# A graph kernel's pre-activations taken from PSUM by one ScalarE copy, with VectorE's sums a piece later in SBUF, and f1 left in a PSUM bank

## The chip, the cores and the metric

The kernel runs on one core of a Trainium2 chip. The metric is the device time of one execution, in microseconds. An engine is named as the profile names it: PE is TensorE, DVE is VectorE, ACT is ScalarE, POOL is GpSimd, SP is SyncE (here it only issues DMAs); PEld is PE's weight load. SBUF is the on-chip memory, PSUM the banks into which PE writes its products, 128 partitions by 512 float32 numbers each.

## What is computed

The input x has 32 entries of 512 nodes by 256 features; adj is one sparse 512 by 512 adjacency matrix with weights. Four layers follow one another; layers 0 and 3 are the same function with different weights, and they are the ones the change is about:

```python
def gnn(h, A, W1, b1, W2, b2, Wa, ba, Wm, bm, beta1, beta2, beta3):   # layers 0 and 3
    pre_u = einsum('bud,dk->buk', h, W1[:d])
    pre_v = einsum('bvd,dk->bvk', h, W1[d:])
    hidden = relu(pre_u[:, :, None, :] + pre_v[:, None, :, :] + b1)
    S = sigmoid(einsum('buvk,ko->buvo', hidden, W2)[..., 0] + b2[0])
    a = einsum('buv,bud->bvd', S * A, h)
    m = einsum('uv,bud->bvd', A, h) * h
    return beta1 * h + beta2 * (a @ Wa + ba) + beta3 * (m @ Wm + bm)

x = gnn(x, adj, ...)                                   # layer 0
x = x + relu((adj @ x) @ W.T + b)                      # layer 1
feats = x @ W1.T; f1 = feats @ W2 + b2                 # layer 2
coefs = softmax(leaky_relu(f1[:, :, None] + f1[:, None, :]) + adj)
x = coefs @ feats + bias2 + x
x = gnn(x, adj, ...)                                   # layer 3
```

S is needed only where adj is not zero: at the edges. The kernel computes it there alone.

## The kernel before

The 32 entries are worked on in eight groups of four (`NB = 4`). A group goes through five streams of work:

- `first` (layer 0, one entry after the other): x is loaded (h0), turned by PE (`turned`, L536) and copied to hT by ACT (L537), stored for later (the DMA xT<-hT, L730), and then `pre` computes pre_u and pre_v.
- `edges` of layer 0: POOL fetches rows of pre_v, one row for each edge and all four entries at once, by an indirect DMA (`fetch`, L582, rows<-table); the partner rows of pre_u come as "mine" by SP (L622) or POOL. DVE adds the two (L654, 128x1024) and takes relu, times W2, summed over features (L667, four times 128x256). After a few items ACT takes exp (L567) and DVE the sigmoid (L571, L572) and the product with the edge's weight (L611), and POOL puts the result into a dense table of cells by an indirect DMA (`put`, L576).
- `middle`: SP loads the dense cells (`load`, L689, SA<-cells), and for each entry `middle_one` does the rest of layer 0, layers 1 and 2, and at its end `pre` for layer 3, from the entry's xT.
- `edges` of layer 3, the same as before with other weights.
- `last`: the rest of layer 3, and the store to the output.

`pre` (L540) is where the change lies. For each of the four chunks of 128 nodes, which the texts call a piece, PE writes pre_u and pre_v side by side into one PSUM tile (pst, 128x512). Then, in order: DVE writes pre_u + b1 into an SBUF tile puv (L549, reading PSUM); ACT copies pre_v into its other half (L550, reading PSUM); DVE adds pre_v, from PSUM, and pre_u + b1 (L552); DVE takes relu, times W2, summed (L553), for the diagonal of S. The DMA that writes puv to the table in HBM (L557, issued by SP) is kept in `self.later` and given out by `settle` at the next piece. There are 8 groups x 2 layers x 4 entries x 4 chunks = 256 pieces. puv has three buffers, shared by `first` and `middle`; `both` has one.

In `middle_one`, f1 (layer 2, one number for each node, spread over the partitions) is written by PE into a PSUM tile and copied to SBUF by ACT (L835); four ACT instructions for each entry read it (L851), each followed by DVE's leaky_relu (L852).

How the order comes about: the streams are Python generators. `sparse_path` gives each of their pieces a share of work, and each stream a start and an end in units of a group's period; `weave` sorts all pieces by the time that follows. Streams marked "fill" (`first`, `last`) are not given out at their time but held, up to eight pieces, and put in where `middle` says that PE would stand still. So `first` of the next group and `last` of the former one run beside `middle` and `edges`. A framework then takes the instructions, orders them for each engine by what it expects of their times, and puts in the semaphores; each engine and each DMA queue works through its own list in order. An instruction that has to wait therefore holds all that stands behind it on its engine. The texts use "boundary" for the place in each period where `first` of the next group ends and the edges of layer 0 begin.

Of the kernel before, what the change touches and what calls it, by code (L numbers as in the profile page):

```python
# [8 lines left out]
F32 = mybir.dt.float32  # L9
# [3 lines left out]
ALU = mybir.AluOpType  # L13
AX = mybir.AxisListType
PSUM = bass.MemoryType.PSUM

P = 128
N = 512
D = 256
NC = N // P  # L20
DC = D // P
# [18 lines left out]
def mm(nc, out, pairs):  # L40

    for n, (lhsT, rhs) in enumerate(pairs):
        nc.tensor.matmul(out, lhsT, rhs, start=(n == 0), stop=(n == len(pairs) - 1))  # L43


class Model:


    def __init__(self, ctx, tc, a):
        nc = self.nc = tc.nc  # L50
        self.tc, self.a = tc, a
        const = self.const = ctx.enter_context(tc.tile_pool(name="const", bufs=1))
        self.ident = const.tile([P, P], F32, name="ident")
        make_identity(nc, self.ident)
        self.adj = const.tile([P, NC, N], F32, name="adj")
        for c in range(NC):
            nc.sync.dma_start(self.adj[:, c, :], a["adj"][c * P : (c + 1) * P, :])
        self.g0, self.g3 = self.gnn_first("L0_gnn"), self.gnn_first("L3_gnn")
# [352 lines left out]
def by_two(t, n=2):  # L411
    return t.rearrange("p (c d) -> p c d", c=n)


class Sparse:
# [3 lines left out]
    def __init__(self, ctx, m, counts, xr, outr, B):  # L419
        self.m, self.nc, self.tc, self.counts = m, m.nc, m.tc, counts  # L420
        tc = m.tc
        self.xr, self.outr = xr, outr
        pool = lambda n, b, **k: ctx.enter_context(tc.tile_pool(name=n, bufs=b, **k))
        self.dram = pool("dram", 1, space=bass.MemoryType.DRAM)

        self.cells = {
            k: [self.dram.tile([CELLS + SPARE, NB], F32, name=f"cells_{k}{q}") for q in range(2)] for k in "03"
        }
        self.lists = self.dram.tile([N, 2 * N], F32, name="lists")
        self.x2s = self.dram.tile([B, P, NC, D], F32, name="x2s")  # L430

        self.xT, self.x2T = (self.dram.tile([B, P, DC, N], F32, name=n) for n in ("xT", "x2T"))
        self.e = Edges(m, pool("edges", 1))
        self.adjT = pool("adjT1", 1).tile([P, NC, N], F32, name="adjT")
        self.grp = pool("grp", 2)
        self.act, self.small, self.gath = pool("act", 1), pool("small", 2), pool("gath", 5)
        self.ps = pool("ps", 8, space=PSUM)
        self.later, self.bigs, self.given = None, 0, None

    def psum(self):  # L440
        return self.ps.tile([P, N], F32, name="pst", tag="pst")
# [97 lines left out]

    def pre(self, g, b, hT):  # L540

        nc, w = self.nc, g.w
        rows = g.table.rearrange("(c p k) (b d) -> p c k b d", p=P, k=2, b=NB)
        for c in range(NC):
            cs = slice(c * P, (c + 1) * P)
            pp = self.psum()
            mm(nc, pp, [(hT[:, d, cs], w["W1"][:, d::DC, :]) for d in range(DC)])
            puv = self.small.tile([P, 2, D], F32, name="puv", bufs=3)
            nc.vector.tensor_tensor(puv[:, 0, :], pp[:, 0:D], w["b1bc"], ALU.add)  # L549
            nc.scalar.copy(puv[:, 1, :], pp[:, D:])  # L550
            both = self.small.tile([P, D], F32, name="both", bufs=1)
            nc.vector.tensor_tensor(both, pp[:, D:], puv[:, 0, :], ALU.add)  # L552
            nc.vector.scalar_tensor_tensor(  # L553
                both, both, 0.0, w["W2bc"], ALU.max, ALU.mult, accum_out=g.self_s[:, c, b : b + 1]
            )
            self.settle()
            self.later = lambda c=c, puv=puv: nc.sync.dma_start(rows[:, c, :, b, :], puv)  # L557
            yield

    def settle(self):  # L560
# [226 lines left out]
    def middle_one(self, g0, g3, b, i, SA, keep, given):  # L787
        nc, m, w = self.nc, self.m, g0.w
        act, small, psum = self.act, self.small, self.psum
# [34 lines left out]
        yT = act.tile([P, DC, N], F32, name="yT")  # L824
# [4 lines left out]
            nc.vector.tensor_tensor(yT[:, c, :], yT[:, c, :], zT[:, c, :], ALU.add)  # L829
            yield c == DC - 1  # L830

        f1 = small.tile([P, N], F32, name="f1", bufs=1)
        pf = psum()
        mm(nc, pf, [(m.q_bc[:, c, :], yT[:, c, :]) for c in range(DC)])
        nc.scalar.copy(f1, pf)  # L835
        feats = act.tile([P, NC, D], F32, name="feats", tag="mhT0")
        eT = act.tile([P, NC, N], F32, name="eT")
        if more:
# [443 lines left out]
```

## Time and profile before

| | |
|---|---|
| median of 3 runs | 3247.94 us (3246.24 to 3251.05) |
| the profiled execution, its own time | 3230.9 us |
| its span in the profile | 3229.2 us |
| granted TensorE clock, mean | 0.928 |
| table<-puv, 256 issues of 256 KB: issue to landing | 2.4 us least, 4.9 median, 15.1 most |

The profile is of one execution. Its page gives the busy time of each engine, the chain of work that ended last, and groups of instructions: line, engine, operation, output tile <- input tile, shapes, count, then the busy time in us and the mean of one in ns, then the idle time of the engine just before them and what ended it. "<-DVE puv L549 376.2" in a row of ACT means: ACT stood idle for 376.2 us in all before these instructions, until a DVE instruction of L549 was done. SPq is SP's queue, the place where DMA issues wait.

### The profile page before, as it was taken

The numbers are of one execution on the slowest core, as the hardware profiler recorded it, in microseconds if no ns is written. First come the engines' busy times: TensorE is split into PE (matmuls) and PEld (weight loads), VectorE is DVE, ScalarE is ACT, GpSimd is POOL, SyncE is SP. The second block draws the span as 40 slices with busy tenths as digits, with TensorE's granted clock in tenths as the row PEclk, the third lists the DMA queues.
The fourth block names the chain that finished last, engine by engine and source line by source line (L and its number), as shares of the span: only waits on it lengthen the run. The fifth ranks groups of instructions, "written<-read, shape, count | busy, mean of one in ns | idle before, by whom it ended". The sixth has DMA issues, their size and how long they took to land.

```text
span 3229.2 us, 32451 instructions
## 1 busy us (share of the span) xinstructions
PE 2773.2 (86%) x8646; PEld 1656.2 (51%) x8646; DVE 2371.6 (73%) x7692; ACT 1007.0 (31%) x2341; POOL 1488.3 (46%) x1248
## 2 busy tenths in 40 slices
PE   6346887989997999979999899979998899999947
PEld 3223444546554566435654565536654465545626
DVE  7777736989596976969598786969688695953662
ACT  4452333322233222333223232333223222232441
POOL 1565402747264543636354462636355362630371
PEclk9677898999999999989999999989999999999969
DMA  8876425777567766776577766776577765640663
GB/s 273 295 246 229 152 91 166 261 262 224 188 226 240 234 196 202 249 241 220 173 230 235 245 203 211 237 250 207 178 219 246 242 221 190 219 159 33 209 201 112
DMA packets 302718, 679.40 MB, mean 210 GB/s; under 512 B 52672, under 2 KB 170944, under 8 KB 294336
## 3 DMA queue, kind: packets, MB, share of 16 engines
q0 software_dynamic: 111168, 338.90, 32.8%
q1 hardware_dynamic: 186224, 334.68, 31.0%
q10 hardware_dynamic: 5136, 3.68, 0.4%
q8 instruction: 71, 1.16, 0.1%
q14 instruction: 119, 0.97, 0.1%
HBM read 531.12 MB, written 146.01 MB: 210 GB/s over the span
## 4 chain that ended last, share of the span: by engine, by line
PE 38%; DVE 34%; DMA 17%; issue 6%; ACT 3%; POOL 1%; SPq 0%; ACTq 0%; POOLq 0%; DVEq 0%
PE pst L43 28%; DVE rows L667 11%; DVE rows L654 10%; DMA rows<-table,iv 6%; DMA table<-puv 4%; PE pst L945 4%; PE pst L802 2%; DMA cells<-s,cell 2%; PE pst L954 1%; DVE ex L852 1%; PE pst L896 1%; DMA cells<-self_s 1%; PE pst L809 1%; DVE ex L854 1%; DMA mine<-table,iu 1%
## 5 line engine op out<-in xcount | busy, mean ns | idle before, releaser
L582 POOL DMA_INDIRECT rows<-table,iv x554 | 680.1, 1228 | 1047.4 <-DMA table<-puv 383.1
L576 POOL DMA_INDIRECT cells<-s,cell x576 | 684.3, 1188 | 592.7 <-DMA cells<-s,cell 357.0
L654 DVE TENSOR_TENSOR rows<-rows,mine 128x1024 f32<-128x1024 f32 x554 | 667.3, 1215 | 195.0 <-DMA rows<-table,iv 178.9
L667 DVE SCALAR_TENSOR_TENSOR rows<-rows,L_gnn_W2bc 128x256 f32<-128x256 f32 x2016 | 750.9, 413 | 0.4
L43 PE MATMUL pst<-adj,h 128*128 128x512 f32 x1024 | 453.5, 592 | 0.0
L43 PE MATMUL pst<-L_gnn_Wa,hT 128*128 128x256 f32 x1024 | 260.6, 408 | 142.4 <-DMA hT<-xT 69.4
L43 PE MATMUL pst<-w_L_gnn_W,hT 128*128 128x512 f32 x512 | 261.2, 646 | 57.4 <-ACT hT L537 46.3
L43 PEld LDWEIGHTS pst<-adj,h 128*128 128x128 f32 x1024 | 192.8, 190 | 219.5 <-issue 214.1
L43 PEld LDWEIGHTS pst<-L_gnn_Wa,hT 128*128 128x128 f32 x1024 | 207.8, 208 | 187.8 <-issue 103.2
L43 PE MATMUL pst<-w_L_gnn_W,yT 128*128 128x512 f32 x512 | 239.9, 622 | 66.0 <-DVE yT L874 66.0
L43 PE MATMUL pst<-eT,feats 128*128 128x512 f32 x512 | 240.0, 624 | 9.1 <-ACT eT L897 9.1
L43 PE MATMUL pst<-adjT,zW 128*128 128x512 f32 x512 | 225.9, 592 | 0.0
L550 ACT COPY puv<-pst 128x256 f32<-128x256 f32 x256 | 94.7, 372 | 412.5 <-DVE puv L549 376.2
L945 PEld LDWEIGHTS pst<-hWa,SA 128*128 128x128 f32 x896 | 213.4, 328 | 5.9 <-issue 3.3
L945 PE MATMUL pst<-hWa,SA 128*128 128x256 f32 x896 | 216.2, 397 | 0.0
L43 PEld LDWEIGHTS pst<-w_L_gnn_W,yT 128*128 128x128 f32 x512 | 101.8, 200 | 196.3 <-issue 111.0
L549 DVE TENSOR_TENSOR puv<-pst,bc_L_gnn_b 128x256 f32<-128x256 f32 x256 | 106.6, 417 | 127.4 <-PE pst L43 64.4
L771 ACT COPY flat<-SA 128x512 f32<-128x512 f32 x128 | 134.5, 1122 | 203.3 <-PE pst L43 178.8
L802 PE MATMUL pst<-flat,hWa 128*128 128x512 f32 x448 | 196.8, 592 | 0.0
L43 PEld LDWEIGHTS pst<-w_L_gnn_W,hT 128*128 128x128 f32 x512 | 102.0, 206 | 168.0 <-issue 90.5
L43 PE MATMUL pst<-WT,hT 128*128 128x256 f32 x512 | 141.8, 434 | 38.8 <-DVE hT L810 38.8
L896 PE MATMUL pst<-ident,ex 128*128 128x128 f32 x512 | 88.5, 302 | 99.2 <-DVE ex L857 62.6
(167 smaller groups left out, 3728.0 us busy)
## 6 DMA issues: line engine op xcount, KB each, us to landing
table<-puv SPq DMA_DIRECT2D x256, 256.0 KB, 4.9
SA<-cells SPq DMA_DIRECT2D x64, 1024.0 KB, 7.0
h<-in_x_dram SPq DMA_DIRECT2D x64, 512.0 KB, 6.6
mine<-table SPq DMA_DIRECT2D x64, 512.0 KB, 6.2
hT<-xT SPq DMA_DIRECT2D x36, 512.0 KB, 5.0
h<-x2s SPq DMA_DIRECT2D x36, 512.0 KB, 6.1
xT<-hT SPq DMA_DIRECT2D x32, 512.0 KB, 7.5
x2T<-yT SPq DMA_DIRECT2D x32, 512.0 KB, 5.0
```

Of the source, the lines that this page charges most:

```text
L43: nc.tensor.matmul(out, lhsT, rhs, start=(n == 0), stop=(n == len(pairs) - 1))
L549: nc.vector.tensor_tensor(puv[:, 0, :], pp[:, 0:D], w["b1bc"], ALU.add)
L550: nc.scalar.copy(puv[:, 1, :], pp[:, D:])
L576: self.nc.gpsimd.indirect_dma_start(out=g.cells[half], out_offset=bass.IndirectOffsetOnAxis(ap=at, axis=0), in_=s, in_offset=None)
L582: self.nc.gpsimd.indirect_dma_start(out=rows, out_offset=None, in_=g.table, in_offset=bass.IndirectOffsetOnAxis(ap=at, axis=0))
L654: nc.vector.tensor_tensor(rows, rows, other, ALU.add)
L667: nc.vector.scalar_tensor_tensor(part, part, 0.0, w["W2bc"], ALU.max, ALU.mult, accum_out=at)
L771: self.nc.scalar.copy(flat[:, r, :], SA[r][:, :, b])
L802: nc.tensor.matmul(pz, hWa[:, r, cs], flat[:, r, :], start=(r == 0), stop=False)
L809: nc.tensor.matmul(pz, w["Wm"][:, d, cs], mhT[:, d, :], start=False, stop=(d == DC - 1))
L896: nc.tensor.transpose(pt[:, js], ex[:, js], self.m.ident)
L945: nc.tensor.matmul(pz[:, k * D : (k + 1) * D], SA[r][:, cs, b], hWa[:, r, :], start=(r + k == 0), stop=False)
```

## The change

In `pre`, ACT now copies the whole 128x512 tile from PSUM to puv, in one instruction in place of the 128x256 copy. DVE's three operations read and write SBUF alone; the first adds b1 to the copied pre_u in place. All three, with the DMA issue between them, are now in `behind`, which `settle` gives out at the next piece (or at the end of the stream). The last reader of the PSUM tile is thus ACT.

In `middle_one`, f1 stays in PSUM: PE writes it into a bank of its own (pool ps_f1), and the four ACT instructions read it there. The pool of all other PSUM tiles has seven banks in place of eight.

```diff
-        self.ps = pool("ps", 8, space=PSUM)
+        self.ps = pool("ps", 7, space=PSUM)
+        self.ps_f1 = pool("ps_f1", 1, space=PSUM)
...
     def pre(self, g, b, hT):
...
+        def behind(c, puv):
+            nc.vector.tensor_tensor(puv[:, 0, :], puv[:, 0, :], w["b1bc"], ALU.add)
+            nc.sync.dma_start(rows[:, c, :, b, :], puv)
+            both = self.small.tile([P, D], F32, name="both", bufs=1)
+            nc.vector.tensor_tensor(both, puv[:, 0, :], puv[:, 1, :], ALU.add)
+            nc.vector.scalar_tensor_tensor(
+                both, both, 0.0, w["W2bc"], ALU.max, ALU.mult, accum_out=g.self_s[:, c, b : b + 1]
+            )
+
         for c in range(NC):
             cs = slice(c * P, (c + 1) * P)
             pp = self.psum()
             mm(nc, pp, [(hT[:, d, cs], w["W1"][:, d::DC, :]) for d in range(DC)])
             puv = self.small.tile([P, 2, D], F32, name="puv", bufs=3)
-            nc.vector.tensor_tensor(puv[:, 0, :], pp[:, 0:D], w["b1bc"], ALU.add)
-            nc.scalar.copy(puv[:, 1, :], pp[:, D:])
-            both = self.small.tile([P, D], F32, name="both", bufs=1)
-            nc.vector.tensor_tensor(both, pp[:, D:], puv[:, 0, :], ALU.add)
-            nc.vector.scalar_tensor_tensor(
-                both, both, 0.0, w["W2bc"], ALU.max, ALU.mult, accum_out=g.self_s[:, c, b : b + 1]
-            )
+            nc.scalar.copy(puv, by_two(pp))
             self.settle()
-            self.later = lambda c=c, puv=puv: nc.sync.dma_start(rows[:, c, :, b, :], puv)
+            self.later = lambda c=c, puv=puv: behind(c, puv)
             yield
...
-        f1 = small.tile([P, N], F32, name="f1", bufs=1)
-        pf = psum()
-        mm(nc, pf, [(m.q_bc[:, c, :], yT[:, c, :]) for c in range(DC)])
-        nc.scalar.copy(f1, pf)
+        f1 = self.ps_f1.tile([P, N], F32, name="f1")
+        mm(nc, f1, [(m.q_bc[:, c, :], yT[:, c, :]) for c in range(DC)])
```

## The prediction

> **What bounds the kernel now.** I read the page's busy shares first, then its chain of waits, then the groups, then short windows of one group's period.
>
> ```profile
> PE 2773.2 (86%) x8646; PEld 1656.2 (51%) x8646; DVE 2371.6 (73%) x7692; ACT 1007.0 (31%) x2341; POOL 1488.3 (46%) x1248
> PE 38%; DVE 34%; DMA 17%; issue 6%; ACT 3%; POOL 1%; SPq 0%; ACTq 0%; POOLq 0%; DVEq 0%
> ...
> L550 ACT COPY puv<-pst 128x256 f32<-128x256 f32 x256 | 94.7, 372 | 412.5 <-DVE puv L549 376.2
> ...
> L549 DVE TENSOR_TENSOR puv<-pst,bc_L_gnn_b 128x256 f32<-128x256 f32 x256 | 106.6, 417 | 127.4 <-PE pst L43 64.4
> ```
>
> PE is nearly full, yet the chain lies on PE for only 38%, on DVE for 34% and on DMA for 17%: the limit changes hands within each group of four entries. The two groups that the change touches look costly: ACT stood idle 376.2 us for DVE's L549. But an average says nothing about worth, so I read the windows (columns: stretch, length, then busy time of PE, PEld, DVE, ACT, POOL, then granted clock, DMA share, GB/s).
>
> ```profile
> 1224.00:1243.00 19.00, 19.00 (x59) 10.33 (x58) 6.78 (x21) 4.76 (x10) 4.77 (x5) 1.00 0.78 223
> 1313.00:1331.00 18.00, 17.71 (x48) 8.09 (x47) 11.54 (x42) 6.94 (x11) 9.01 (x9) 1.00 0.76 259
> 1331.00:1350.00 19.00, 15.82 (x38) 6.83 (x37) 19.00 (x69) 2.62 (x5) 11.71 (x11) 0.99 0.68 217
> 1372.00:1385.00 13.00, 11.51 (x47) 6.83 (x45) 12.45 (x49) 7.45 (x19) 7.04 (x7) 1.00 0.31 79
> 1385.00:1400.00 15.00, 8.81 (x24) 4.86 (x25) 6.02 (x23) 5.67 (x13) 1.94 (x2) 0.77 0.95 341
> 1400.00:1428.00 28.00, 15.99 (x48) 8.35 (x47) 8.46 (x25) 7.19 (x11) 6.20 (x7) 0.82 0.89 280
> ```
>
> A group's period is about 370 us (the last piece of `middle` starts its L549 at 859.35 and at 1229.48). Where DVE waits at L549 or L552 in 1224 to 1243, PE is full: those waits cost nothing there. From 1331 to 1372 DVE is full and PE starves a little. From 1385 to 1428 neither works: PE is busy 24.8 of 43 us, and this "boundary", where `first` of the next group ends and its edges begin, is a chain of latencies. Three lines carry it: the timeline on DVE, ACT and PE.
>
> ```profile
> 1390.96 0.42 DVE L549 TENSOR_TENSOR puv<-pst,bc_L_gnn_b 128x256 f32<-128x256 f32 x1 [6.46 <-DMA table<-puv]
> 1390.56 1.07 ACT L537 COPY hT<-pst 128x512 f32<-128x512 f32 x2 [7.73 <-DMA xT<-hT]
> 1426.28 4.64 PE L43 MATMUL pst<-w_L_gnn_W,yT 128*128 128x512 f32 x5 [11.28 <-DVE yT L874]
> ```
>
> The first waits for one of three puv buffers, whose transfer lands 8 to 10 us after its issue. The second waits for the xT store, which SP issued only at 1382.37, because SP stood at L689 (the load of SA) until the cells were put:
>
> ```profile
> 1370.72 1.87 SPq L557 DMA_DIRECT2D table<-puv  x2
> 1381.95 0.33 SPq L689 DMA_DIRECT2D SA<-cells  x1
> 1382.37 0.38 SPq L730 DMA_DIRECT2D xT<-hT  x1
> ```
>
> The third waits behind L654, whose rows are fetched once the last table piece lands (about 1415).
>
> **The change part by part.** All sums are made against the profiled run, 3230.9 us (span 3229.2), which is 17.0 us under the median of 3247.94; I carry the difference over to the median.
>
> *ACT's work.* 256 copies grow from 128x256 (372 ns) to 128x512. The row of that shape is L835's:
>
> ```profile
> L835 ACT COPY f<-pst 128x512 f32<-128x512 f32 x32 | 18.8, 587 | 84.7 <-PE pst L43 84.7
> L851 ACT ACTIVATE ex<-f,cols 128x512 f32<-128x512 f32 x128 | 91.1, 718 | 48.8 <-DVE cols L849 48.5
> L828 ACT ACTIVATE yT<-pst,col_L_gnn_b 128x512 f32<-128x512 f32 x64 | 43.8, 685 | 135.9 <-PE pst L43 135.9
> ```
>
> 256 x 0.215 = +55.0 us; L835's 32 copies go, -18.8; L851 then reads PSUM as L828 does, 128 x (685 - 718) = -4.2. In all +32 us on an engine busy 1007 of 3229: beside other work, at zero by itself. Uncovered it would be 32 us. The removed f1 copy shortens yT, f1, ex by up to 0.59 us in each of 32 entries, mostly under a full PE: bounds 0 and -19, I take -2.
>
> *DVE's work.* Its three operations per piece stay; two of them now read SBUF twice instead of PSUM and SBUF.
>
> ```profile
> L829 DVE TENSOR_TENSOR yT<-yT,hT 128x512 f32<-128x512 f32 x64 | 43.9, 685 | 66.2 <-ACT yT L828 66.2
> L957 DVE TENSOR_TENSOR h<-pst,h 128x512 f32<-128x512 f32 x64 | 43.5, 680 | 20.2 <-PE pst L954 20.1
> ```
>
> 5 ns dearer at twice the length: 512 x 2.5 ns = 1.3 us, taken as 0. The page "SBUF — State Buffer" of the Trainium skill, section "Who interferes with whom", speaks against this: a VectorE instruction with both inputs in SBUF contends with a GpSimd instruction that reads SBUF, and whoever is second blocks. With POOL busy 46% and half of its 1.23 us instruction to wait, an estimate by it is 512 x 0.46 x 0.6 = +141 us of DVE time; the two rows above, taken beside the same POOL work, differ by 5 ns and show none of that.
>
> What does cost is order. The L552 to L553 neighbours, of which the second needs the first, start 0.459 us apart in the timeline, independent ones 0.333 to 0.346: +0.12 us each. In the changed program's order, add and sum stand next to one another 74 times (they were parted by the ACT copy before) and sum and the relu 88 times against 53: (74 + 35) x 0.12 = +13 us, of which I put half into DVE-bound stretches: +6 (bounds 0, +13).
>
> *Waits that go.* L549's 64.4 us for PE and 61.2 for buffers, L552's 41.0 for ACT, ACT's 376.2 for DVE. In each period they pay at two spots. First, the end of `middle` (1224 to 1243): DVE's next L654 waits for rows, these for the last table piece, this for L549, a 0.59 us copy of L887 in front of L550 on ACT, L550, and two x2s issues in front of it on SP. At the last group the trace shows it wholly on the chain: matmul end 3016.26, L549 3016.46, L550 3017.38, issue 3018.69. The new order has the piece's copy ahead of L887's and its issue ahead of the x2s: copy 3016.47 to 3017.06, add to 3017.5, issue 3017.55, so 1.1 us earlier, 8 times, less a little: **-8**. Second, 1313 to 1331: DVE stands 4.58 us at L549 for a buffer with work behind it, and PE is then short of 3.2 us in the next stretch. In the new order ACT stands there and DVE goes on with rows; but ACT feeds PE too. Bounds 0 and -27 (six times 4.58), I take -5.
>
> *Moved and added.* The table issue of a piece now needs DVE's add, which is given out one piece later. I laid the two DVE orders side by side and summed the row durations of other DVE work between the old place of L549 and the new place of the add: median 1.4 us, up to 4.9 within `first`. Against the time that each buffer had to spare before its next writer (that start less the landing), 43 pieces fall short, by 80 us together. ACT pays these waits now, with hT (L537), feats, exp and eT copies queued behind, for which PE waits.
>
> SP's order moves too. From the fourth group on, the first SA load of layer 3 stands two table pieces, an hT load and an h load earlier. In before, the two pieces went at 1370.72 and the SA load held SP until 1381.95; after, the pieces, the hT load and the xT store stand behind that wait, hold two of the three buffers until about 1390, and stop ACT at the next copy with some 3 us of its work behind it (two copies, a feats, two exps). The hT copies, now at 1390.56, come about 3 us later, PE's 1391.19 batch with them, and so the last table piece and L654. Five boundaries x 3 = **+15** (bounds 0, if the puts end earlier because DVE no longer stands still; +40 at 8 each). On the other side, the puts may come some us earlier, as sigmoid pieces no longer stand behind a stopped L549.
>
> In `middle` the fourth piece's issue now stands behind up to seven other SP issues (h1, mine, hT1, hT3, out, h3, an SA0 load), some 75 us later; its buffer is next wanted about then, so 0 to +2 us of ACT each, under a full PE: 0. POOL's order keeps its fetches behind all table pieces of their group.
>
> *PSUM.* Seven banks and one for f1. From the first matmul to the last reader of each pst tile, seven or more live for only 22 us, all between 84 and 110; later the smallest spare time with seven is 2.8 us. Bounds 0 and +10, I take +2.
>
> Sum: -2 + 6 - 8 - 5 + 15 + 2 = **+8 us**; 3247.94 + 8 = 3256.
>
> **Rivals.**
> 1. *Faster: DVE's waits were real.* If ACT's new waits fall where PE is fed anyway, the gains stay: -8, -27, and a part of the PE idle behind ACT's hT copies, which the page gives as 46.3 us; with half of that, and +13 and +2 against it, -43: about 3205 to 3235. For it: DVE is 34% of the chain, and ACT's 376.2 us of waiting for DVE go. Against: they lie mostly beside a full PE. It decides where ACT's stops stay under 2 us.
> 2. *Slower by more: ACT becomes the slot's hostage.* One mechanism at one place, the stopped copy in front of hT, feats and eT. If half of the 80 us and all of the +40 reach PE, +80; half of that is likelier: 3275 to 3300. It decides from a buffer wait of about 3 us on ACT, above which PE's queue of ready work (2.8 us of spare banks) runs out. For it: the 7.73 us that ACT already waits there show PE stopped 6.92 us.
> 3. *Nothing:* waits change places only; 3248. For it: PE 86% and an ACT with 69% to spare.
>
> **How the numbers follow.** The forecast (+7 to +25) gets 0.36, rival 1 0.35, rival 2 0.15, rival 3 0.14. About 0.2% (6.5 us) is what a measurement of this kernel can tell from no change. So faster 0.35, same 0.14, slower 0.51. Signs are mixed; the forecast's own range is 3255 to 3273. The whole range goes from 3210 (most of rival 1) to 3290 (most of rival 2).
>
> **What would show it.** L561's copy near 590 ns and some 80 us of waits on "DMA table<-puv", on ACT instead of DVE; DVE's waits on ACT and PE shorter; L654 in the last group about 1 us earlier after its matmul; SP at the SA load with table pieces behind it; PE's gap before the hT batch at the boundary 8 to 10 us instead of 6.92. I am wrong if ACT's waits for buffers come to under 20 us, if the SA load finds its puts done, if DVE's SBUF adds take clearly over 420 ns, or if PE's idle time shrinks by over 20 us.

## The result, and the profile after

The changed kernel takes 3275.53 us (median of 4 runs, 3273.10 to 3281.85) against 3247.09 (4 runs, 3245.31 to 3251.05) on the same chip: the ratio is 1.0094, with a 95% interval of 1.0080 to 1.0109, or some 26 to 35 us. The profiled execution of the changed kernel has a span of 3276.2 us. That of before (3229.2) lay 17 us under its median. The experiments ran in three batches (e1 to e4, e5 to e8, e9 to e12), each on another chip, on which before takes 3228 to 3230 us (median), so only ratios are compared between batches. Where the trace of the changed kernel is laid beside that of before, some 2 of 370 us in each period may come from that.

Page of the changed kernel: busy time first, then the groups of ACT's copy, of DVE's addition of b1 and of the rows add.

```profile
PE 2781.5 (85%) x8645; PEld 1656.9 (51%) x8646; DVE 2375.8 (73%) x7692; ACT 1034.2 (32%) x2309; POOL 1456.0 (44%) x1248
...
L660 DVE TENSOR_TENSOR rows<-rows,mine 128x1024 f32<-128x1024 f32 x554 | 666.9, 1217 | 252.6 <-DMA rows<-table,iv 229.3
...
L561 ACT COPY puv<-pst 128x512 f32<-128x512 f32 x256 | 147.3, 583 | 376.6 <-PE pst L43 178.2
...
L548 DVE TENSOR_TENSOR puv<-puv,bc_L_gnn_b 128x256 f32<-128x256 f32 x256 | 107.7, 422 | 166.9 <-ACT puv L561 166.1
```

The work costs what it was taken to cost: 583 ns a copy, ACT 1034.2 us (+27), DVE 2375.8 (+4). The waits have moved. ACT's 376.2 us of waiting for DVE are gone. DVE's waits at a piece were 166.6 us before: 64.4 for PE, 61.2 for a buffer, 41.0 for ACT. They are 166.1 after, now all for ACT. The lists of waits show it (who waited for what, total, times, longest), first two lines of before, then two of the changed kernel:

```profile
DVE puv L549 <- DMA table<-puv: 61.2, 26, 6.5
DVE both L552 <- ACT puv L550: 41.0, 54, 1.8
```

```profile
ACT puv L561 <- PE pst L43: 178.2, 103, 12.4
...
ACT puv L561 <- DMA table<-puv: 142.4, 36, 17.3
```

So ACT now waits 142.4 us for one of the three puv buffers, where DVE had waited 61.2. Of the 142.4 us, 59.1 lie in the first 883 us, ahead of the five periods that are compared below; in before it was 10.2. The boundary shows what such a wait does. First SP's queue there, in the changed kernel:

```profile
1386.85 4.87 SPq L549 DMA_DIRECT2D table<-puv  x2
1403.84 0.34 SPq L695 DMA_DIRECT2D SA<-cells  x1
1404.28 1.81 SPq L549 DMA_DIRECT2D table<-puv  x1
1406.14 0.60 SPq L788 DMA_DIRECT2D hT<-xT  x1
1406.83 0.51 SPq L549 DMA_DIRECT2D table<-puv  x1
1407.44 0.61 SPq L905 DMA_DIRECT2D h<-x2s  x1
1408.14 0.70 SPq L736 DMA_DIRECT2D xT<-hT  x1
...
1423.64 0.33 SPq L695 DMA_DIRECT2D SA<-cells  x1
1424.06 0.38 SPq L736 DMA_DIRECT2D xT<-hT  x1
1424.54 1.63 SPq L549 DMA_DIRECT2D table<-puv  x2
```

The first SA load waits for the cells until 1403.84. Two table stores, an hT load, an h load and the xT store stand behind it; the two pieces had been copied at 1395.26 and 1397.47 and added to at 1396.47 and 1398.32. At 1423.64 goes the third of the four SA loads, again with table stores behind it. Then ACT's timeline at the same place, and PE's, in the changed kernel and in before:

```profile
1409.89 0.58 ACT L561 COPY puv<-pst 128x512 f32<-128x512 f32 x1 [4.55 <-DMA table<-puv]
...
1418.65 0.58 ACT L561 COPY puv<-pst 128x512 f32<-128x512 f32 x1 [3.79 <-DMA table<-puv]
1419.13 1.08 ACT L538 COPY hT<-pst 128x512 f32<-128x512 f32 x2
...
1432.99 0.58 ACT L561 COPY puv<-pst 128x512 f32<-128x512 f32 x1 [3.80 <-DMA table<-puv]
```

```profile
1419.78 2.93 PE L43 MATMUL pst<-w_L_gnn_W,hT 128*128 128x512 f32 x3 [9.00 <-ACT hT L538]
```

```profile
1391.19 3.44 PE L43 MATMUL pst<-w_L_gnn_W,hT 128*128 128x512 f32 x4 [6.92 <-ACT hT L537]
```

ACT stands at two copies with the hT copies queued behind them, and PE stands 9.00 us where it had stood 6.92. The hT copies also needed the xT store, which landed at 1415.44 here, so at most 3.69 of the 9.00 us are ACT's stop. This boundary is the longest stand of the five in both kernels: as a mean over five boundaries PE stands 8.13 us where it had stood 4.96. Behind the third SA load ACT stops once more (3.80 us at 1432.99), in four of the five boundaries; before has no stop there.

To see where a period gains and loses, I number DVE's rows adds (72 in a period, 36 for each layer) and take the time from one to another, as a mean over the five periods in the middle of the run. The second column is the boundary, the gap between the last add of layer 3's edges and the first of layer 0's; the fourth is the gap at the end of `middle`. An edge stretch that ends later makes the boundary behind it look shorter, so the first two columns are read together. The last column says behind which of the next group's 16 table stores the four SA loads of layer 3 stand in SP's order; it is the same in all five periods.

```
kernel                  edges of 3  boundary  edges of 0  end of middle  period  SA loads
before, us                   128.6      50.8       125.5           65.8   370.7  8, 9, 13, 16
the whole change              +1.0      +5.7        -0.4           +2.0    +8.3  6, 8, 11, 13
e1  f1 only                   -0.2      -2.1        -1.0           +2.0    -1.2  9, 11, 15, 16
e2  pre only                  +0.7      +5.8        +0.5           +1.0    +7.9  7, 9, 11, 14
e3  four buffers              +0.2      +3.1        -1.7           +1.5    +3.1  6, 8, 11, 13
e4  sums at once              +0.0      +4.3        -2.6           +2.9    +4.6  6, 8, 11, 13
e5  order, start              -1.5      +6.4        -0.2           +1.2    +5.9  7, 9, 11, 14
e6  order, all                +4.9      +0.9        +4.7           -0.4   +10.0  7, 9, 11, 13
e7  e6, four buffers          +3.4      +0.4        +4.7           -0.8    +7.7  7, 9, 11, 13
e8  before, four buffers      -1.8      -0.5        -0.3           +2.6     0.0  9, 11, 15, 16
e9  SP order                  +0.9      +0.4        -0.4           +2.3    +3.3  8, 9, 13, 16
e10 e9, four buffers          +0.2      +1.3        +0.5           +1.6    +3.6  8, 9, 13, 16
e11 before, sums behind       -0.4      +4.7        -2.7           +3.7    +5.2  8, 9, 11, 14
e12 mildest form              -0.5      +0.3        -1.6           +3.0    +1.1  8, 9, 13, 16
```

### The profile page after: what moved, and what is told of

It reads as the page before. It is cut to its first block, busy times and chain, and to the rows that moved or that the text cites. A ratio compares the mean times of both kernels' runs of the same rounds, so it can differ in the third digit from the quotient of the medians.

```text
span 3276.2 us, 32240 instructions
## 1 busy us (share of the span) xinstructions
PE 2781.5 (85%) x8645; PEld 1656.9 (51%) x8646; DVE 2375.8 (73%) x7692; ACT 1034.2 (32%) x2309; POOL 1456.0 (44%) x1248
## 5 line engine op out<-in xcount | busy, mean ns | idle before, releaser
L588 POOL DMA_INDIRECT rows<-table,iv x554 | 653.1, 1179 | 1070.9 <-DVE rows L673 259.2
L673 DVE SCALAR_TENSOR_TENSOR rows<-rows,L_gnn_W2bc 128x256 f32<-128x256 f32 x2016 | 752.3, 418 | 0.2
L561 ACT COPY puv<-pst 128x512 f32<-128x512 f32 x256 | 147.3, 583 | 376.6 <-PE pst L43 178.2
L548 DVE TENSOR_TENSOR puv<-puv,bc_L_gnn_b 128x256 f32<-128x256 f32 x256 | 107.7, 422 | 166.9 <-ACT puv L561 166.1
L573 ACT ACTIVATE s<-s,L_gnn_nb 128x16 f32<-128x16 f32 (+2 forms) x176 | 53.6, 305 | 466.8 <-DVE rows L673 465.6
```

The source lines that it names most:

```text
L548: nc.vector.tensor_tensor(puv[:, 0, :], puv[:, 0, :], w["b1bc"], ALU.add)
L561: nc.scalar.copy(puv, by_two(pp))
L573: self.nc.scalar.activation(t, t, AF.Exp, bias=w["nb2"], scale=-1.0)
L588: self.nc.gpsimd.indirect_dma_start(out=rows, out_offset=None, in_=g.table, in_offset=bass.IndirectOffsetOnAxis(ap=at, axis=0))
L673: nc.vector.scalar_tensor_tensor(part, part, 0.0, w["W2bc"], ALU.max, ALU.mult, accum_out=at)
```

## The experiments

Two theories stood against each other. The **buffer theory** is the prediction's: stores late in SP's queue hold the puv buffers, ACT stops at its copy with work behind it. The **order theory** came from laying the traces side by side: in the changed kernel DVE's instructions of `middle` stand one or two rows adds later in DVE's queue. At the end of `middle` it looks striking. DVE's timeline of the changed kernel:

```profile
1263.37 1.23 DVE L660 TENSOR_TENSOR rows<-rows,mine 128x1024 f32<-128x1024 f32 x1 [11.79 <-DMA rows<-table,iv]
1264.51 0.68 DVE L718 TENSOR_TENSOR mhT<-pst,hT 128x512 f32<-128x512 f32 x1
1266.49 2.35 DVE L660 TENSOR_TENSOR rows<-rows,mine 128x1024 f32<-128x1024 f32 x2
1268.76 0.68 DVE L718 TENSOR_TENSOR mhT<-pst,hT 128x512 f32<-128x512 f32 x1
```

The product mhT, which PE needs, waits behind an add that waits 11.79 us for its rows. In before it had gone first, and the add had idled 4.58:

```profile
1237.25 0.69 DVE L712 TENSOR_TENSOR mhT<-pst,hT 128x512 f32<-128x512 f32 x1 [4.50 <-PE pst L43]
1242.52 1.23 DVE L654 TENSOR_TENSOR rows<-rows,mine 128x1024 f32<-128x1024 f32 x1 [4.58 <-DMA rows<-table,iv]
```

The expectations give some ranges in microseconds; they mean a chip on which before takes 3247.

### e1 and e2: the two parts alone

e1 takes f1's lines of the diff and the two pools, and leaves `pre`. e2 takes `pre`, and leaves f1's copy and the eight banks.

> Only the f1 part of the change: f1 stays in its own PSUM bank, seven banks for the rest, pre as before. Buffer theory (the loss is ACT's waits for puv buffers, 142 us in the changed kernel, and SP's order) and order theory (the loss is that DVE's instructions of middle now stand one or two edge items later in DVE's queue) both expect no loss here: 3240 to 3250 against 3247 for before. If seven banks cost something, 3255 or more.

Measured: 1.0012 (0.9997 to 1.0027). The f1 part is worth nothing clear of noise either way, and seven banks cost nothing that shows. Its columns are not all zero, though: SP's order moves with f1 too, the boundary is 2.1 us shorter and the gap at the end of `middle` 2.0 us longer than in before.

> Only the pre part: the whole copy by ACT and the sums a piece behind in SBUF, f1 copied by ACT as before, eight banks. Both theories expect the whole loss here, 3270 to 3280; a clearly smaller loss would mean that the f1 bank shares in it.

Measured: 1.0114 (1.0093 to 1.0134), ACT's waits for buffers 164.3 us. The whole loss is in `pre`.

### e3 and e4: a fourth buffer, and the sums at once

```diff
-            puv = self.small.tile([P, 2, D], F32, name="puv", bufs=3)
+            puv = self.small.tile([P, 2, D], F32, name="puv", bufs=4)
```

> The changed kernel with four puv buffers in place of three. Buffer theory: most of ACT's 142 us of waits for table<-puv go, and with them most of the 28 us: 3248 to 3258. Order theory: DVE's order of middle against the edge items is as in the changed kernel, so the waits for buffers go and the time stays within 8 us of it, 3267 to 3276.

Measured: 1.0074 (1.0057 to 1.0090); ACT's waits for buffers fall from 142.4 to 60.6 us.

```diff
             nc.scalar.copy(puv, by_two(pp))
+            nc.vector.tensor_tensor(puv[:, 0, :], puv[:, 0, :], w["b1bc"], ALU.add)
+            both = self.small.tile([P, D], F32, name="both", bufs=1)
+            nc.vector.tensor_tensor(both, puv[:, 0, :], puv[:, 1, :], ALU.add)
+            nc.vector.scalar_tensor_tensor(
+                both, both, 0.0, w["W2bc"], ALU.max, ALU.mult, accum_out=g.self_s[:, c, b : b + 1]
+            )
             self.settle()
-            self.later = lambda c=c, puv=puv: behind(c, puv)
+            self.later = lambda c=c, puv=puv: nc.sync.dma_start(rows[:, c, :, b, :], puv)
```

> The changed kernel with VectorE's three sums given out right after the copy instead of a piece behind; the table store stays a piece behind as in before. Buffer theory: buffers are free as early as in before, waits for them fall to some 60 us and the time to 3247 to 3258. Order theory: two thirds of the shift in DVE's order remain (mhT's products stand 32 edge items later in sum instead of 44), so about two thirds of the loss: 3262 to 3270.

Measured: 1.0058 (1.0041 to 1.0074), buffers 118.2 us. On a chip where before takes 3247, e3 would be 3271 and e4 3266: both lie in the ranges of the order theory and outside those of the buffer theory. Four buffers take away more than half of the waits but only a fifth of the loss: 0.20 of 0.94%, with intervals that overlap. Sums at once take away 0.36%, clear of the intervals, and the waits that remain are double those that the buffer theory expected. The order theory was ahead at this point.

### e5 to e7: DVE's order put back

An edge of order alone, without a wait, puts a rows add behind an instruction of `middle` on DVE. e5 does so for the two mhT products of a group's first entry, before the first and the third rows add; e6 for mhT, zT, yT and xT in all groups, at the places of before; e7 is e6 with four buffers.

```diff
+            near = self.turns[k // 2 - 2] if g.last and k in (0, 2) else None
+            with self.tc.issue_after(near) if near is not None else ExitStack():
-            nc.vector.tensor_tensor(rows, rows, other, ALU.add)
+                nc.vector.tensor_tensor(rows, rows, other, ALU.add)
```

> The changed kernel with one piece of DVE's order put back: the two products mhT of each group's first entry stand again before the first and before the third rows add of layer 3's edges, as in before; all else as in the changed kernel. Order theory: the loss between the end of one group's middle and its next first entry (5 to 6 us in each of six periods, +33 us in the trace) goes for the most part: 3245 to 3255 where before runs at 3247, ratio 1.000 to 1.003. Buffer theory: nothing changes, ratio 1.008 to 1.010.

Measured: 1.0114 (1.0097 to 1.0132), far outside the order theory's range. The place itself was cured: between the x2T stores of a group's last entry and of the next group's first, the trace is 0.9 us slower than before where the whole change was 4.6 (stores at 1220 and 1316 in before). But the boundary takes +6.4 us instead of +5.7, and nothing is gained in sum.

> The changed kernel with DVE's order of mhT, zT, yT and xT against the rows adds put back to that of before in all groups; three puv buffers. Order theory: ratio to before 0.998 to 1.003. Buffer theory: the waits of ACT for buffers (142 us) stay and so does the loss, ratio 1.007 to 1.010. If both have a share, about 1.004.

Measured: 1.0201 (1.0180 to 1.0223), above every range that was expected.

> The same order put back, and four puv buffers. Each theory alone expects what its own cure gives: buffer theory 1.007 as with four buffers alone, order theory the same as with the order alone. If the two add up (order -30 us at the start of middle, buffers -15 us at the boundary), it ends below before: ratio 0.995 to 0.999.

Measured: 1.0164 (1.0147 to 1.0181), above every range that was expected.

The order theory falls as a theory of the loss: with before's order of `middle` on DVE the kernel is slower still. Both edge stretches, where DVE is full, are longer by 4.9 and 4.7 us. The boundary is +0.9 us only because the adds in front of it end later: with the edges of layer 3 it makes +5.8, where e2 has +6.5. The test is not clean either, since SP's order is not that of before in e6 (last column), so the runs show that this order doesn't mend the changed kernel, and not why it costs another 1.1%. With buffers added to it (e7), 0.37% comes back, more than at the order of the changed kernel.

### e8: four buffers for before

Before with f1 in its bank, and four puv buffers in the room that f1 leaves.

> Before with f1 in its PSUM bank and, in the room that this frees, four puv buffers; pre as in before, so DVE's order is that of before. If puv buffers bound the boundary in before as well (DVE waited 61 us for them), 0.996 to 0.999 of before; if DVE's waits lie beside a full PE, 0.999 to 1.002.

Measured: 0.9991 (0.9979 to 1.0003). DVE's waits for buffers fall from 61.2 to 28.7 us, and the interval of the ratio holds 1: against before, the half of these waits that went is worth at most 0.21%. Against e1, which has f1 in its bank too (72.8 us of such waits, 1.0012), the ratio is 0.21% lower, with intervals that overlap. That is the size of e3's gain, so a worth of nothing is not shown.

### e9 and e10: SP's order put back

The SA loads of layer 3 are issued behind the same table pieces of the next group as in before (the 8th, 9th, 13th and 16th):

```diff
+            ahead = self.stores[(7, 8, 12, 15)[c]] if layer == 3 and len(self.stores) == 16 else None
+            with self.tc.issue_after(ahead) if ahead is not None else ExitStack():
-            self.nc.sync.dma_start(t.rearrange("p v b -> p (v b)"), cells.rearrange("(p v) b -> p (v b)", p=P))
+                self.nc.sync.dma_start(t.rearrange("p v b -> p (v b)"), cells.rearrange("(p v) b -> p (v b)", p=P))
```

> The changed kernel with SP's order at the boundary put back: each of layer 3's four SA loads is issued behind the same table piece as in before; three puv buffers, DVE's order as in the changed kernel. Buffer theory with the prediction's SP step (plus 15 us): the two pieces and the hT load no longer stand behind the wait for the cells, the boundary's gap on DVE falls by 3 to 6 us of the 5.7 that it grew in each period, and the time by 15 to 30 us: ratio to before 1.001 to 1.005. If the wait on SP is not the cause, ratio 1.008 to 1.011 as for the whole change.

Measured: 1.0078 (1.0054 to 1.0101). This lies between the two ranges that were expected, at the edge of the one for "not the cause" (1.008 to 1.011). At the boundary itself the queue does what was expected of it. SP's queue in e9, and PE's gap before the hT batch:

```profile
1380.40 0.34 SPq L796 DMA_DIRECT2D hT<-xT  x1
1381.85 2.35 SPq L551 DMA_DIRECT2D table<-puv  x2
1388.32 0.33 SPq L701 DMA_DIRECT2D SA<-cells  x1
1388.74 0.80 SPq L744 DMA_DIRECT2D xT<-hT  x1
```

```profile
1398.85 2.07 PE L43 MATMUL pst<-w_L_gnn_W,hT 128*128 128x512 f32 x2 [4.00 <-ACT hT L540]
```

The hT load and the two stores go ahead of the SA load, PE waits 4.00 us instead of 9.00 (4.35 instead of 8.13 as a mean over five boundaries), the stop behind the third SA load is gone in all five, and the boundary is back at +0.4 us. The nearest code is the whole change, and against its 1.0094 the gain is 0.16%, inside the intervals. Against e2 (f1 copied, on another chip) the period falls from +7.9 to +3.3 and the time from 1.0114 to 1.0078, by 0.36%. So the gain at the boundary is plain in the trace, its worth in time is 0.16 or 0.36% by which run it is compared with, and it is not the whole.

> SP's order put back and four puv buffers. If both act on the same stalls of ACT, no more than either alone, 1.001 to 1.005; if they add, 0.998 to 1.001. If what is left comes from DVE's order or from the sums behind, it stays at 1.003 or above.

Measured: 1.0066 (1.0042 to 1.0089). Buffers add 0.12% to the order, inside the intervals. The result falls in the third case that was set down: 1.003 or above, what is left comes from DVE's order or from the sums behind. ACT's waits for buffers are 27.4 us here, less than DVE's 61.2 in before, and 0.3 us in the five boundaries together, so little speaks for them as the remaining 0.66%.

### e11: the sums behind, and nothing else

Before, with the two later sums alone put a piece behind, in SBUF; the copy stays half and after DVE's addition.

```diff
             nc.vector.tensor_tensor(puv[:, 0, :], pp[:, 0:D], w["b1bc"], ALU.add)
             nc.scalar.copy(puv[:, 1, :], pp[:, D:])
-            both = self.small.tile([P, D], F32, name="both", bufs=1)
-            nc.vector.tensor_tensor(both, pp[:, D:], puv[:, 0, :], ALU.add)
-            nc.vector.scalar_tensor_tensor(
-                both, both, 0.0, w["W2bc"], ALU.max, ALU.mult, accum_out=g.self_s[:, c, b : b + 1]
-            )
             self.settle()
-            self.later = lambda c=c, puv=puv: nc.sync.dma_start(rows[:, c, :, b, :], puv)
+            self.later = lambda c=c, puv=puv: behind(c, puv)
```

> Before with the two later sums alone put a piece behind, reading SBUF; the addition of b1 and ACT's half copy read PSUM as in before, f1 is copied, eight banks, three buffers. The table store waits for nothing new. DVE's 41 us of waits for ACT go. If DVE's waits at a piece were worth their time, ratio 0.990 to 0.996; if they lie beside other work or are paid elsewhere, 0.998 to 1.003.

Measured: 1.0100 (1.0073 to 1.0127), a miss, and a telling run. The sums behind lose as much as the whole change, without the whole copy and without the late addition of b1. The 41 us do not even go: DVE still waits 45.5 us for ACT at the sums, and its waits for buffers rise from 61.2 to 105.2. The boundary is part of it; DVE's timeline and SP's queue:

```profile
1401.31 0.42 DVE L557 TENSOR_TENSOR puv<-pst,bc_L_gnn_b 128x256 f32<-128x256 f32 x1 [8.97 <-DMA table<-puv]
1419.25 0.43 DVE L557 TENSOR_TENSOR puv<-pst,bc_L_gnn_b 128x256 f32<-128x256 f32 x1 [8.45 <-DMA table<-puv]
```

```profile
1394.63 1.32 SPq L545 DMA_DIRECT2D table<-puv  x2
1409.49 0.32 SPq L692 DMA_DIRECT2D SA<-cells  x1
1409.91 0.37 SPq L733 DMA_DIRECT2D xT<-hT  x1
1410.71 2.64 SPq L545 DMA_DIRECT2D table<-puv  x3
```

Here it is the third SA load that moved ahead of table stores: in before five stores stood between the first SA load and the third, here three. The piece copied at 1401.81 is stored at 1410.71, and DVE stands 8.45 us. So a change in where DVE's work of a piece stands moved SP's order too.

Such a stop behind the third SA load sets the runs apart. In all eight runs whose third SA load stands behind the 11th table store (the whole change, e2 to e7, e11), ACT or DVE stops for a buffer behind that load, in three to five of the five boundaries, and edges of 3 and boundary are together 3.3 to 6.7 us longer than in before. In the six where it stands behind the 13th or the 15th there is no such stop, and the two are together between 2.3 us shorter and some 1.5 us longer. The first SA load, to which the prediction looked, does not separate them: in e11 it stands where before has it, and in e2 the hT load is ahead of it and PE's gap before the hT batch is 5.35 us in the mean (4.96 in before), and both boundaries are long. No run moved the third load alone.

### e12: the mildest form

Whole copy, sums at once, f1 in its bank, SP's order put back, four buffers.

> The mildest form of the change: whole copy by ACT, sums at once, f1 in its bank, SP's order at the boundary put back, four puv buffers. If the loss is made of late stores, of buffers and of SP's order, nothing of it is left: ratio 0.996 to 1.001. If ACT's longer copy in front of its other work costs by itself, 1.003 to 1.006.

Measured: 1.0023 (1.0008 to 1.0037). This lies between the two ranges that were expected and decides for neither. Waits for buffers are down to 21.3 us, the boundary is at +0.3, and 0.71 of the 0.94% is gone. e10 is the same kernel but for the sums, which are a piece behind there, on the same chip and with the same SP order at the boundary: 1.0066 against 1.0023. So the late sums cost 0.43% even where neither SP's order at the boundary nor many waits for buffers stand behind it. No version beat before clearly; e8 is the nearest.

## Why the prediction was right in its direction and too small

Forecast were +8 us with an own range of +7 to +25, measured some +28; the whole range of 3210 to 3290 held, and it was wide enough for a gain as well. Slower had been given 0.51, little better than a toss. The time lies just inside rival 2's range (3275 to 3300), which had been given 0.15, and rival 2's mechanism, the copy stopped in front of the hT copies, is what the trace shows at the boundary: ACT stops there for 3 to 5 us at a time. Point by point:

- **ACT's and DVE's durations** were right: 583 ns for 587; the two sums that now read SBUF twice take 422 and 419 ns for 417 and 418. On "SBUF — State Buffer" of the Trainium skill, section "Who interferes with whom" (a VectorE instruction with two SBUF inputs contends with a GpSimd one that reads SBUF): with POOL busy 44%, these 512 instructions became 1 to 5 ns longer, and DVE's unchanged L667 (L673 after) became 5 ns longer too (413 to 418), so no blocking of the size that I had worked out from it shows here. Whether POOL's indirect DMAs read SBUF in the page's sense no run here shows.
- **f1 and the banks**: -2 and +2 were taken, 0 together; e1 shows 1.0012, with 1 inside its interval.
- **SP's order at the boundary**, +15, was the right kind of mechanism, found in the queues before the run, and right in half of its place. PE's gap before the hT batch was to be 8 to 10 us instead of 6.92 and is 9.00; in the mean of five boundaries it grew by 3.2 us, which is the 3 us for a period that were taken. But the boundary grew by 5.7 (5.8 in e2): I had looked at the first SA load alone, and not at the third, behind which ACT stops again. e9 puts all four loads back and takes the boundary to +0.4, so it confirms SP's order as the cause at this place, and not which load it is.
- **ACT's waits for buffers**: 80 us were expected, 142.4 came. Some 59 of them lie in the first groups, where before has 10.2. The stores behind the SA loads explain only a part: with SP's order put back (e9) 120.6 us remain. Where the others come from is not shown.
- **The end of middle**, -8: the 1.1 us were won as worked out, and did not arrive. From the first instruction of the first piece (DVE's addition in before, ACT's copy after) to the last store it took 6.27 us instead of 7.38, and in the last group the last store went 1.32 us behind the matmul's end instead of 2.43. But from the last store to the first rows add it then took 13.2 us instead of 11.2 (mean of five), and in the last group that add stood 14.29 us behind the matmul's end instead of 13.97. The longer way from store to add is in every run with the whole copy (12.2 to 13.2 us) and in none with the half copy (11.2 to 11.3); what slows the fetch there (it now starts closer behind the x2s and mine transfers) no run tells apart. The +2.0 us of the column cannot be laid to the pieces: e1 and e8, with the pieces of before, have +2.0 and +2.6.
- **DVE's stop at 1313 to 1331**, -5, gave nothing that shows: the edge stretch that holds it is 1.0 us longer, not 4.6 shorter. What was not seen is that DVE, where ACT stands, waits for ACT: at this place 1.97, 0.82 and 0.34 us instead of 4.58, and 166.1 us in the whole run. The sign "DVE's waits on ACT shorter" failed with it (41.0 before). So did rival 1, for which ACT's stops had to stay harmless.
- **The sums behind** were no step of the prediction by themselves; I had priced their neighbourhood on DVE (+6) and the late addition. e11 shows that moving two instructions a piece back is enough for a loss as large as the whole (1.0100). In the other direction giving the sums at once takes away 0.36% (e4 against the whole change, on different chips) and 0.43% (e12 against e10). SP's order at the boundary is the same within each of these two pairs, so it cannot be the whole way in which late sums cost time.

What stays open: e9 leaves 0.78% with a boundary that is nearly as short as in before, and the periods account for some 16 of its 25 us. The runs show shares: sums behind 0.36 and 0.43%; a fourth buffer 0.12 to 0.37%; SP's order 0.16 or 0.36%. They overlap, and those of the buffer and of SP's order are for the most part not clear of noise. All three together leave 1.0023. By which way the late sums cost time where SP's order and the buffers are put right (e10) is not shown. The whole copy, with the longer way from the last store to the rows add that goes with it, was not run alone with before's queues.

## What to carry to other kernels

A wait that an engine loses can turn up on the engine that took over the work: look for it at the same place (166.6 and 166.1 us here), and not at the one line that vanished. Nor is the sum of waits a price: in e10 DVE's waits at a piece are 95.6 us, and the kernel is still 0.66% slower than before. Before moving an instruction "a piece behind", list what a buffer's release and each queue's order hang on; a store behind a load that waits for something else holds its buffer for that whole wait. And a local cure is worth only what the next place down the chain lets through: the mhT order was mended in e5 at its place, and in sum nothing was gained.

## What the runs showed that was not expected

The order in which the framework sets DVE's instructions was not the weak point that it seemed to be: forcing that of before on the changed kernel cost another 1.1% (1.0201 against 1.0094). And two small VectorE instructions, given out one piece later and nothing else (e11), cost 1.0% (1.0073 to 1.0127), with DVE's waits for buffers up from 61.2 to 105.2 us.
